# A two-layer decoder on one core: the fold of the second layer's experts moves into the end of the first layer's attention, and the gather of expert rows moves into the next stage's batch loop

## The chip, the cores and the metric

The kernel runs on one core of one Trainium2 chip. The core has TensorE (PE in the profile, with PEld for its weight loads), VectorE (DVE), ScalarE (ACT), GpSimd (POOL) and SyncE (SP, which here only issues DMAs). Each engine takes its instructions in the order of its own queue. The metric is the device time of one execution in microseconds (us).

## The reference, cut to what matters

Two decoder layers over x of 4 batches x 512 tokens x 256 channels, float32. Each layer is attention, cross attention, experts, each on a layer norm of x and added back to x:

```
x += L0_attn(LN(x))        # causal conv, 16 heads, cumulative memory
x += L0_xattn(LN(x), ctx)  # 16 heads, softmax over 512 keys
x += L0_ffn(LN(x))         # 12 experts, 2 per token: 8 with silu, 4 that pass x through
x += L1_attn(LN(x))        # gated scan over time: f = LN(x) @ W_f.T, scan, @ W_down.T
x += L1_xattn(LN(x), ctx)  # ternary weights, int8 activations
x += L1_ffn(LN(x))         # 8 linear experts, 2 per token: (x @ w_in[e].T) @ w_out[e].T
```

Two facts carry the change. The experts of the last line have nothing between their two matrices, so the product of w_in[e] (1024 x 256) and w_out[e] (256 x 1024) is a matrix of 256 x 256 that depends on weights alone; the kernel calls it the fold of expert e, and may compute it at any moment before the last stage. And the sum over a token's two experts in L0_ffn ends in a gather: each token fetches two rows out of a table in device memory and adds them, weighted by its shares, to its x.

## The kernel before, in words

Tokens lie on the 128 partitions, in 16 tiles (NT) of 128 tokens, 4 (QT) per batch. The stages run in the order of the list FAST: `l0_mixers` (both attentions of layer 0), `l0_gate`, `ahead`, `l0_experts`, `l1_attn`, `l1_xattn`, `l1_ffn`. A library orders the instructions of each engine when the kernel is built: it simulates the program, takes the first one in program order that is ready, and adds the waits. `keep_in_program_order` pins an instruction behind the one that was written before it for the same engine. Memory pools are handed out like a stack; what is put where another tile was waits until that tile's last use.

**l0_mixers.** After a prologue, a loop over 17 units u = 0..16 computes cross attention scores, four units to a batch. A unit has eight slots n = 0..7. In each slot `exponents` (from L912) does two score matmuls into one of two PSUM buffers, a DVE maximum (L917) and two ACT exponentials (L920), after which the buffer is free again. The dictionary `then` holds what is done behind each slot: for the unit before, `least` and `weigh` in slots 1 and 2 (small matmuls on PE, then DVE, ACT and a POOL product, L943), `gather_values` in slots 3 to 6 (eight `av` matmul instructions in each, which need that POOL product). SP fetches the next unit's keys and queries (`gather`, slot 0) and values (slot 4). The remaining slots of the first ten units do the first attention's work for later batches. In units 10 and 14 `project` puts one output projection (`xo`, eight matmul instructions of 128x256) in each of slots 4 to 7. Unit 16 has no scores; its tail is `collect` (the softmax sums go to device memory), `invert`, `give_back`, `spread` (eight DMAs and POOL products, L996) and `project` for batch 3, one behind the other. All matmuls here go through `pinned` and all SP DMAs through `move`, so PE and SP keep the written order. Single-bank PSUM tiles come from `ps_misc`, which has four banks.

**l0_gate.** Per batch: layer norm, turn, gate matmuls on PE, top two on DVE, and the row numbers; then POOL writes the normalized rows into the table by indirect DMAs (L1346), 32 in all.

**l0_experts.** `take(e)` loads an expert's weights and its 640 rows, `expert(e)` computes `ef` matmuls (shape 128x320, then 128x256) and writes the rows back (L1431). Beside it run `weights` (seven ternary weight matrices, DVE and SP), `images` (work for l1_xattn) and `fold` (L1710), a generator: for each of eight experts two 1 MB loads, 32 matmul instructions of 128x256, an ACT copy and a 256 KB write to `far_folded`. Its first steps are interleaved with `weights`, the rest are written last. Behind the experts stands the gather: for each of 16 tiles and two picks, an indirect DMA by POOL into `got` (six buffers, L1453) and one multiply-add into x on DVE (L1459).

**l1_attn.** For each batch: layer norm, eight PE transposes (`turn`), copies to `aht`; then for m = 0, 1, 2 four `f` matmuls (twice as many instructions, of 128x512), three ACT sigmoids, two DVE operations, a POOL product (L1531) and a DVE scan (L1532); then the `down` matmuls and the DVE addition to x (L1537).

**l1_ffn** reads `far_folded` near the end of the kernel.

Of the kernel before, what the change touches and what calls it, by code (L numbers as in the profile page):

```python
# [9 lines left out]
F32 = mybir.dt.float32  # L10
# [8 lines left out]
P = 128  # L19
# [521 lines left out]
def l0_mixers(k):  # L541
# [19 lines left out]
    k.close_psum()  # L561
    with ExitStack() as es:
        pool = lambda n, bufs, **kw: es.enter_context(tc.tile_pool(name=n, bufs=bufs, **kw))
        wp, wk, sp = pool("l0_w", 1), pool("l0", 2), pool("l0_s", 3)
        ps_misc, ps_s = pool("l0_misc", 4, space=PSUM), pool("l0_score", 2, space=PSUM)
# [26 lines left out]
        def load(name, src=None):  # L592
            src = a[name] if src is None else src
            t = wp.tile(list(src.shape), F32, name=f"{name}_sb")
            move(t, src)
            return t

        def load_rows(name):
            return load(name, a[name].rearrange("(c p) f -> p c f", p=P))

        def load_all(name):
            return load(name, a[name].to_broadcast([P, a[name].shape[1]]))
# [37 lines left out]
        gamma = wp.tile([16, 1], F32, name="gamma_sb")  # L640
# [10 lines left out]
        half_b = wp.tile([P, 4], F32, name="half_b")  # L651
# [12 lines left out]
        power = wp.tile([16, 10], F32, name="power")  # L664
        decay_of = []
        nought = wp.tile([1, P], BF16, name="nought")
        far_dec = dram.tile([2, 16, T], F32, name="far_dec", bufs=1)
        near_dec = wp.tile([P, 2, 64], F32, name="near_dec")
# [29 lines left out]
        cos = wp.tile([P, 4, T], F32, name="cos")  # L698
# [22 lines left out]
        def normalize(b):  # L721
            normal[b] = k.layer_norm(b)
            mixed[b] = wk.tile([P, DC, T], F32, tag="xc", name=f"xc_{b}", bufs=1)
# [24 lines left out]
        def measure(b, m):  # L748

            if m == 0:  # L750
                raw[b] = wk.tile([P, 4, T], F32, tag="qk", name=f"qk_{b}", bufs=1)
# [6 lines left out]
        heads = wp.tile([P, 4, 16], F32, name="heads")  # L758
# [16 lines left out]
        def scale_near(b):  # L775
            rn = near_of[b] = wk.tile([P, 3, 64], F32, tag="rn", name=f"rn_{b}", bufs=1)
# [13 lines left out]
        def factor(b, m):  # L790

            two = factor_of[b, m] = wk.tile([P, 2, T], F32, tag="factors", name=f"factors_{b}_{m}")
            by_channel(two, lambda r: factors[b][r, m])

        def gated_values(b, m):
# [6 lines left out]
            vg = gated[b, m] = wk.tile([P, T], F32, tag="vg", name=f"vg_{b}_{m}", bufs=4)  # L802
# [201 lines left out]

        def blank(n):
# [69 lines left out]
        w_o = load_rows("Wo")  # L1075
        b_o = load_all("bo")
# [49 lines left out]
        for u in range(units + 1):  # L1126
# [17 lines left out]
            near_b, next_b, last_b = b + 1, b + 2, b + 3  # L1144
            if m == 0:
# [59 lines left out]
        give_back(NB - 1)  # L1205
        for half in range(2):
            spread(NB - 1, half)
        for i in range(QT):
            project(NB - 1, i)
# [845 lines left out]
```

## Time and profile before

| what | us |
|---|---|
| median of 3 executions (lowest, highest) | 1324.41 (1321.67, 1333.49) |
| profiled execution, device time | 1339.99 |
| its span, first to last instruction | 1338.3 |
| l0_mixers, to the last `xo` matmul | 0 to 568 |
| gate and table writes, to the first expert matmul on rows | 569 to 646 |
| experts, to their last write of the table | 646 to 847 |
| gather of rows, to the first `f` matmul | 847 to 913 |
| rest of l1_attn | 913 to 1008 |
| l1_xattn and l1_ffn | 1008 to 1338 |

Of the span PE is busy 76%, DVE 61%, ACT 30%, POOL 16%; the mean granted PE clock is 0.847 of full speed. The 256 fold matmul instructions take 69.0 us of PE, the 32 gathers 31.1 us of POOL. A line of the profile names the source line, engine, operation, what is written and from what, and how many; in a timeline the first two numbers are the start and the duration in us, and the brackets hold the idle time before it and what ended that.

### The profile page before, as it was taken

How to read it: one execution, taken by the hardware profiler on the slowest of the kernel's cores; microseconds unless marked ns; L12 is line 12 of the kernel's file. 1: busy time of each engine (PE TensorE's matmuls, PEld its weight loads, DVE VectorE, ACT ScalarE, POOL GpSimd, SP SyncE). 2: the span in 40 equal slices, each digit the busy share in tenths (PEclk: the TensorE clock that was granted, in tenths of full speed). 3: DMA queues.
4: the chain of work that ended last, by engine and by line, in shares of the span. 5: the costliest groups of instructions: out<-in, count | busy, mean ns of one | idle time of the engine just before them, and what ended most of it. 6: DMA issues, size and time to landing. Idle time of an engine off the chain costs nothing. (4 is left out here: it accounts for less than half of the span.)

```text
span 1338.3 us, 11843 instructions
## 1 busy us (share of the span) xinstructions
PE 1015.5 (76%) x3742; PEld 559.0 (42%) x3742; DVE 812.9 (61%) x1969; ACT 405.0 (30%) x698; POOL 213.9 (16%) x245
## 2 busy tenths in 40 slices
PE   5859668789767667472689999849873788669996
PEld 2434323233323223262566677735441443255442
DVE  6646687787687666162356821254766555887564
ACT  4503246445434564010012321002311343730000
POOL 4421112112112010136000000451112110000000
PEclk9969778889887778665799999869986898979999
DMA  5382712524523230156565352651000011010000
GB/s 150 93 270 92 214 36 104 168 102 149 166 94 118 71 106 0 34 176 216 169 230 163 119 200 75 201 164 40 0 0 4 16 48 32 0 41 24 16 31 19
DMA packets 91885, 132.27 MB, mean 99 GB/s; under 512 B 20853, under 2 KB 62325, under 8 KB 91797
## 3 DMA queue, kind: packets, MB, share of 16 engines
q1 hardware_dynamic: 85648, 113.58, 27.2%
q0 software_dynamic: 6144, 17.83, 3.8%
q8 instruction: 32, 0.52, 0.2%
q14 instruction: 41, 0.33, 0.1%
q10 hardware_dynamic: 20, 0.00, 0.0%
HBM read 88.72 MB, written 42.66 MB: 98 GB/s over the span
## 5 line engine op out<-in xcount | busy, mean ns | idle before, releaser
L920 ACT ACTIVATE e<-score,tops 128x512 f32<-128x512 f32 x256 | 161.2, 685 | 152.0 <-DVE tops L917 103.2
L917 DVE TENSOR_REDUCE tops<-score 128x2 f32<-128x1024 f32 x128 | 155.6, 1220 | 50.5 <-PE score L581 49.8
L212 PE MATMUL y<-folded_sb,fht 128*128 128x512 f32 x256 | 113.0, 601 | 0.0
L581 PE MATMUL score<-query,key 64*128 64x512 f32 x256 | 73.2, 574 | 35.9 <-ACT e L920 34.1
L955 PE MATMUL av<-e,weighed 128*32 128x512 f32 x512 | 84.2, 700 | 19.7 <-POOL weighed L943 19.7
L1911 DVE SCALAR_TENSOR_TENSOR x_sb<-y,tt_w,x_sb 128x256 f32<-128x256 f32 x128 | 61.9, 483 | 38.5 <-PE y L212 34.9
L212 PE MATMUL ef<-sw,eact 128*128 128x256 f32 x320 | 79.9, 389 | 3.2 <-DVE ey L1429 3.2
L212 PE MATMUL fold<-w_out,w_in 128*128 128x256 f32 x256 | 69.0, 423 | 14.2 <-issue 14.2
L581 PEld LDWEIGHTS score<-query,key 64*128 64x128 f32 x256 | 27.2, 212 | 123.4 <-ACT e L920 71.8
L581 PE MATMUL o<-o_wT_sb,qk 128*128 128x256 f32 x128 | 51.0, 567 | 34.6 <-DVE qk L819 34.6
L212 PE MATMUL ef<-eht,sw 128*128 128x320 f32 x256 | 74.6, 435 | 0.6 <-ACT eact L1418 0.6
L212 PEld LDWEIGHTS y<-folded_sb,fht 128*128 128x128 f32 x256 | 48.9, 193 | 60.2 <-issue 60.2
L212 PEld LDWEIGHTS ef<-sw,eact 128*128 128x128 f32 x320 | 58.9, 194 | 13.9 <-DVE ey L1429 6.6
L212 PEld LDWEIGHTS fold<-w_out,w_in 128*128 128x128 f32 x256 | 53.8, 216 | 22.7 <-issue 15.0
L581 PEld LDWEIGHTS o<-o_wT_sb,qk 128*128 128x128 f32 x128 | 35.0, 287 | 49.7 <-DVE qk L819 40.0
L212 PEld LDWEIGHTS ef<-eht,sw 128*128 128x128 f32 x256 | 47.6, 190 | 18.4 <-ACT eact L1418 1.6
L1418 ACT ACTIVATE eact<-ef 128x640 f32<-128x640 f32 x32 | 22.4, 702 | 96.4 <-PE ef L212 96.3
L581 PE MATMUL xo<-Wo_sb,att 128*128 128x256 f32 x128 | 37.1, 439 | 16.8 <-POOL att L996 16.8
L212 PE MATMUL f<-aht,W_fT_sb 128*128 128x512 f32 x96 | 47.7, 645 | 1.4 <-DVE x_sb L1537 1.4
L1453 POOL DMA_INDIRECT got<-table,rows x32 | 31.1, 972 | 104.6 <-DMA table<-ey 94.2
L943 POOL TENSOR_TENSOR weighed<-v,weighed 128x256 f32<-128x256 f32 x16 | 10.5, 658 | 226.8 <-ACT weighed L942 226.8
L1398 PE MATMUL eturn<-ident,rows 128*128 128x128 f32 x80 | 16.9, 295 | 34.6 <-DMA rows<-table 30.8
(376 smaller groups left out, 1811.2 us busy)
## 6 DMA issues: line engine op xcount, KB each, us to landing
table<-zeros POOLq DMA_DIRECT2D x8, 1152.0 KB
factors<-far SPq DMA_DIRECT2D x64, 128.0 KB
key<-far_k SPq DMA_DIRECT2D x16, 512.0 KB
query<-far_q SPq DMA_DIRECT2D x16, 512.0 KB
w_in<-in_w_in SPq DMA_DIRECT2D x8, 1024.0 KB
w_out<-in_w_outT SPq DMA_DIRECT2D x8, 1024.0 KB
rows<-table SPq DMA_DIRECT2D x8, 640.0 KB
table<-ey SPq DMA_DIRECT2D x8, 640.0 KB
```

The source lines that it names most:

```text
L212: self.nc.tensor.matmul(out, lhs_t, rhs, start=(i == 0), stop=(i == len(pairs) - 1))
L581: nc.tensor.matmul(out, lhs_t, rhs, start=start and i == 0, stop=stop and i == len(pairs) - 1)
L917: nc.vector.tensor_reduce(top, ps, AX.X, ALU.max, negate=True)
L920: nc.scalar.activation(e[:, i, :], ps[:, i, :], AF.Exp, bias=top[:, i : i + 1])
L943: weighing[0] = nc.gpsimd.tensor_mul(wt[:, :, :, 0:16], vs[u], wt[:, :, :, 16:17].to_broadcast([P, QT, 4, 16]),)
L955: nc.tensor.matmul(avs[u][32 * h : 32 * h + 32, :], weighed[u % 2][:, j, h, :], es_of[u, h // 2, j][:, h % 2, :], start=(j == 0), stop=(j ...
L1398: nc.tensor.transpose(ps[:, c, :], rows[:, i, c * P : (c + 1) * P], k.ident)
L1418: nc.scalar.activation(act[:, f, :].rearrange("p (j t) -> p j t", j=2), ps[:, :, :half], AF.Silu)
L1453: nc.gpsimd.indirect_dma_start(out=got, out_offset=None, in_=k.table, in_offset=bass.IndirectOffsetOnAxis(ap=k.rows[:, which, t : t + 1], ...
L1911: nc.vector.scalar_tensor_tensor(xt, ps[:, e, :], w[:, i, e4 + e : e4 + e + 1], xt, ALU.mult, ALU.add)
```

## The change

Three things are done.

The fold leaves `l0_experts`. In `l0_mixers`, the tiles of the first attention now come from two pools of their own at the other end of the memory (`mw`, `mt`). At unit 10 (FOLDING) these pools are closed, and a pool `fold_w` for two experts' weights is opened in their place. A fold is cut into four pieces of eight matmul instructions; units 11 to 16 have one behind each of slots 0, 1, 2 and 7, which makes experts 0 to 5. Each fold's first piece also issues the next expert's loads, now four DMAs of 512 KB on SP; its last piece is followed by the ACT copy and the write to `far_folded`. Expert 6 comes behind `give_back` of the tail, expert 7 behind its last `project`. The pieces are pinned like the other matmuls and DMAs there.

The gather leaves `l0_experts`. In `l1_attn`, the 16 row fetches of the first two batches are issued at the start, and the four tiles of batch 0 are added to x before its layer norm. In batch b, behind m = 0 and m = 1, POOL issues the fetches for two tiles each of batch b + 2, and DVE adds two tiles each of batch b + 1. There are 16 `got` buffers instead of six. Fetches, additions and the POOL product are pinned.

`weights` in `l0_experts` is no longer interleaved with anything. The fold for the general path (not executed here) becomes a plain function.

```diff
 def l0_mixers(k):
+    far_folded(k)
+        mixers = ExitStack()
+        mw, mt = (
+            mixers.enter_context(tc.tile_pool(name=n, bufs=bufs, side="right"))
+            for n, bufs in (("l0_mix_w", 1), ("l0_mix", 2))
+        )
...
+        def fetch_fold(e):
+            folds[e] = []
+            for name in ("w_in", "w_outT"):
+                t = k.fold_w.tile([P, 8, D], F32, tag=name, name=f"{name}_{e}", bufs=2)
+                src = a[name][e].rearrange("(c p) d -> p c d", p=P)
+                for j in (0, 4):
+                    move(t[:, j : j + 4], src[:, j : j + 4])
+                folds[e].append(t)
+
+        def fold_piece(i):
+            e, c, j4 = i // 4, i // 2 % 2, i % 2 * 4
+            if i % 4 == 0:
+                folds[e].append(bank(f"fold_{e}").rearrange("p (c d) -> p c d", d=D))
+                if e + 1 < 7:
+                    fetch_fold(e + 1)
+            w_in, w_out, ps = folds[e]
+            pinned(
+                ps[:, c, :],
+                [(w_in[:, j, c * P : (c + 1) * P], w_out[:, j, :]) for j in range(j4, j4 + 4)],
+                j4 == 0,
+                j4 == 4,
+            )
+            if i % 4 == 3:
+                folded = k.fold_w.tile([P, DC * D], F32, tag="folded", name=f"folded_{e}", bufs=2)
+                nc.scalar.copy(folded.rearrange("p (c d) -> p c d", d=D), ps)
+                move(k.far_folded[e], folded)
...
             near_b, next_b, last_b = b + 1, b + 2, b + 3
+            if u == FOLDING:
+                mixers.close()
+                k.fold_pool = ExitStack()
+                k.fold_w = k.fold_pool.enter_context(tc.tile_pool(name="fold_w", bufs=2, side="right"))
+                after(7, fetch_fold, 0)
+            elif u > FOLDING:
+                for j, n in enumerate((0, 1, 2, 7)):
+                    after(n, fold_piece, 4 * (u - FOLDING - 1) + j)
...
         give_back(NB - 1)
+        for i in range(24, 28):
+            fold_piece(i)
         for half in range(2):
             spread(NB - 1, half)
+        fetch_fold(7)
         for i in range(QT):
             project(NB - 1, i)
+        for i in range(28, 32):
+            fold_piece(i)
+    k.fold_pool.close()
     k.open_psum()
...
 def l0_experts(k):
-        folding = fold(k, wf)
             ternary = weights(k, tw)
             take(0)
-            for _ in range(3):
-                for _ in range(2):
-                    next(folding)
-                    next(ternary)
...
-        for t in range(NT):
-            xt = k.x[:, t, :]
-            for which in range(2):
-                got = wk.tile([P, D], F32, tag="got", name=f"got_{t}_{which}", bufs=6)
-                nc.gpsimd.indirect_dma_start(out=got, ...)
-                nc.vector.scalar_tensor_tensor(
-                    xt, got, k.shares[:, which, t : t + 1], xt, ALU.mult, ALU.add
-                )
-        for _ in folding:
-            pass
...
 def l1_attn(k):
+        def fetch(t):
+            for which in range(2):
+                got[t, which] = wk.tile([P, D], F32, tag="got", name=f"got_{t}_{which}", bufs=16)
+                tc.keep_in_program_order(nc.gpsimd.indirect_dma_start(out=got[t, which], ...))
+        def add(t):
+            xt = k.x[:, t, :]
+            for which in range(2):
+                tc.keep_in_program_order(nc.vector.scalar_tensor_tensor(xt, got[t, which], ...))
+        for t in range(2 * QT):
+            fetch(t)
+        for t in range(QT):
+            add(t)
         for b in range(NB):
             h = k.layer_norm(b)
...
-                nc.gpsimd.tensor_mul(g, g, z)
+                tc.keep_in_program_order(nc.gpsimd.tensor_mul(g, g, z))
                 nc.vector.tensor_tensor_scan(state[:, m, :], fade, g, 0.5, ALU.mult, ALU.add)
+                for t in (2 * m, 2 * m + 1) if m < 2 else ():
+                    fetch((b + 2) * QT + t)
+                    add((b + 1) * QT + t)
```

## The prediction

> **What bounds the kernel now.** I read the granted clock first (0.847 on the one core), then busy time in stretches cut at the ends of units, stages and batches, then the timeline of each stretch that the diff touches, then its waits. The stretches, with the columns named in the first line:
>
> ```profile
> core 0: us, PE busy (x) PEld busy (x) DVE busy (x) ACT busy (x) POOL busy (x), PEclk, DMA share, GB/s
> ...
> 423.40:439.60 16.20, 16.20 (x81) 8.24 (x80) 10.77 (x17) 7.59 (x12) 0.23 (x1) 0.97 0.21 75
> ...
> 456.24:473.25 17.01, 11.44 (x53) 3.19 (x53) 10.47 (x13) 10.64 (x18) 0.64 (x1) 0.70 0.20 68
> ...
> 490.26:513.58 23.32, 19.13 (x84) 9.72 (x85) 13.84 (x23) 11.37 (x19) 3.10 (x3) 0.78 0.25 74
> ...
> 646.20:668.90 22.70, 20.57 (x86) 16.73 (x87) 8.78 (x28) 0.58 (x1) 0.00 (x0) 0.85 0.49 156
> ...
> 800.00:846.03 46.03, 46.03 (x205) 36.72 (x204) 8.53 (x17) 5.62 (x8) 0.00 (x0) 1.00 0.21 65
> 846.03:912.76 66.73, 43.54 (x175) 34.64 (x173) 32.66 (x128) 4.10 (x7) 31.10 (x32) 0.77 0.57 183
> ```
>
> The second row is a plain unit (12): 17.0 us, no engine full, PE at clock 0.70. The third is unit 14, with four projections. The experts (fifth) are all PE. The last row is the gather, where no engine is full: a chain. Its timeline:
>
> ```profile
> 846.49 0.36 SPq L1431 DMA_DIRECT2D table<-ey  x1
> 850.62 1.19 POOL L1453 DMA_INDIRECT got<-table,rows  x1 [94.22 <-DMA table<-ey]
> 856.14 0.48 DVE L1459 SCALAR_TENSOR_TENSOR x_sb<-got,shares,x_sb 128x256 f32<-128x256 f32 x1 [9.68 <-DMA got<-table,rows]
> ...
> 891.16 0.95 POOL L1453 DMA_INDIRECT got<-table,rows  x1 [0.30 <-issue]
> 897.48 0.48 DVE L1459 SCALAR_TENSOR_TENSOR x_sb<-got,shares,x_sb 128x256 f32<-128x256 f32 x1
> 904.23 7.81 PE L212 MATMUL fold<-w_out,w_in 128*128 128x256 f32 x32
> 912.76 7.13 PE L212 MATMUL f<-aht,W_fT_sb 128*128 128x512 f32 x16
> ```
>
> POOL issues 32 gathers from 850.62 to 892.1, one per 1.25 to 1.3 us; the first layer norm gets through DVE at 897, and a fold stands in front of the first `f`. So this stretch is paid for by the number of gathers, and the folds in it are only partly free.
>
> **Terms 1 and 2: gather and l1_attn.** The table's last write still lands at 850.6. Batch 0 now needs 8 gathers: the eighth is issued at 850.6 + 7 x 1.25 = 859.4. The first took 5.5 us to its use, beside 2 MB of fold loads which are gone; I take 4, bounds 3 and 5.5, so 863.4. Then addition 0.48, statistics 0.6, ten small operations of 0.2, four `h` of 0.34, turns 2.3, copy 0.7: `f` starts near 871 instead of 912.8. PE comes to it cold (it had been idle, not folding): I charge 2 us. **Term 1: -40.**
>
> From there l1_attn took 95.3 us (912.76 to 1008.03). The product of one m starts 4.03 us behind that of the m before (921.36, 925.40, 929.43). In batches 0 and 1 four gathers are pinned between two products on POOL: 1.27 + 4 x 1.25 = 6.27 us, 2.24 more, twice a batch, 9.0 in all. Behind the product wait the scan and, on DVE's queue, the next m. In batch 2 there are no gathers, but four additions of 0.48 behind the scan: 1.9, twice, 3.8. Layer norms 1 to 3 (about 5 us of DVE each, made beside the gathers before) also come in; DVE is busy about 15 of 22.6 us in a batch, mostly idle behind `down` (5.6 us), so I charge 1 us each. **Term 2: +16**, bounds +6 (only half of the gathers show) and +36 (all additions 11.5, three layer norms 16 and the gathers 9 in the chain).
>
> **Term 3: the experts start earlier.** Between 646.2 and 668.9 fold matmuls take 17.3 us of PE's 20.6. Expert 0's rows are turned by 654.7; its 32 `ef` matmuls were spread until 676.8. Without folds they take 9.2 us, some of them cold (+2): done at 666, 11 earlier. The ternary weights follow more slowly: a 1 MB fold load stood before W_f1's 2 MB load at 669, and the DVE passes over W_f1 (4.42, 2.35, 4.49) hold up the turns as now. I take **-9**. The gain lasts to the end because PE is then full (46.03 of 46.03 in the fifth row). Bounds 0 (weights hold everything) and -11.
>
> **Term 4: units 11 to 15.** Each gets 32 fold instructions, 128x256. The nearest row is the same shape, `xo`, first cold, then warm:
>
> ```profile
> 463.73 1.94 PE L955 MATMUL av<-e,weighed 128*32 128x512 f32 x8 [2.12 <-POOL weighed L943]
> ...
> 500.34 3.26 PE L581 MATMUL xo<-Wo_sb,att 128*128 128x256 f32 x8
> 503.53 1.07 PE L955 MATMUL av<-e,weighed 128*32 128x512 f32 x8
> 504.53 0.50 PE L581 MATMUL score<-query,key 64*128 64x512 f32 x2
> 504.96 1.99 PE L581 MATMUL xo<-Wo_sb,att 128*128 128x256 f32 x8
> ```
>
> A piece costs 2.0 us warm, 3.26 cold. In unit 12 PE idles 1.17, 0.96, 1.02 and 2.12 us behind slots 7, 0, 1 and 2: 5.3 us for 8. Slot by slot, at warm prices: behind 7, a score (0.43) and a piece make 2.45 where 1.67 was (+0.8); behind 0, 2.45 for 1.45 (+1.0); behind 1, with `low`, 2.72 for 1.72 (+1.0); behind 2 the piece hides in the wait for the weighed values (first line). A busier PE is also a faster one: in the stretch 423 to 440, PE full, the clock is 0.97, and `av` takes 1.07 instead of 1.94. The first two `av` groups and a score save 1.9. So +0.9 a unit for 11 to 13. Unit 14 has its projections behind slot 7 too: +3.1. Unit 15: +0.1. **Term 4: +6.** From below: all hidden, clock gain kept, -9. From above: unit 14's four projections lengthened it by 23.3 - 17.0 = 6.3 us; the same for each of five is +31. I stand nearer the lower end because the pieces sit in the idle slots, the projections in the full ones.
>
> [...]
>
> Loads: 2 MB per 17 us unit is 123 GB/s on top of at most 106 GB/s in these units; the stretch from 569 to 587 moved 244 GB/s, so 2 MB takes 8 to 9 us, and each expert is fetched a unit ahead. On SP the loads stand behind the next keys and queries (needed 17 us later) and before the values (needed later still). The first fetch has only its keep writes before it (427.8) and is not late at 440. Charged at nothing; if a load were late, every score behind the piece would wait.
>
> **Term 5: the tail.** Unit 16's gaps (1.63, 0.62, 1.37) take 3.6 of three pieces' 6: +2.2. Piece 23, its copy (0.6) and its 256 KB write are pinned before `collect`, whose DMA went out at 539.68: +2.6, and 1 for the queue. Expert 6's four pieces run while the sums travel (PE idles 12.7 us before 551.7), but its write is pinned before `spread`: +0.5. **+6.3**, bounds 0 and +13 (cold pieces).
>
> **Term 6: the gate.** Expert 7's 32 instructions stand before the gate's turns on PE if its loads are there: at that stretch's price (0.35 each, clock 0.56) 11.2 us, less what PE idles. Against that, fold 0 no longer delays batch 1's ranks, and POOL's gaps of 2.3 and 2.2 us between the table writes close: -4.5. The turns may also slip in between. **+3**, bounds -4.5 and +10.
>
> **Sum:** -40 + 16 - 9 + 6 + 6.3 + 3 = **-17.7 us** against the profiled execution's 1339.99 (span 1338.3). That execution was 15.6 us above the median shown; I carry the difference over: 1324.4 - 18 = **1306**.
>
> **Rivals.**
> *Everything goes well*: units hidden (0), gate -4, the experts -11, l1_attn +11: -40 + 11 - 11 + 0 + 6.3 - 4 = -38, 1286. The long idle of POOL and DVE in the gather speaks for it. Chance 0.15.
> *The experts do not move*: the weights' chain (loads, DVE) sets their pace, term 3 is 0: -9, 1315. For it: PE idled 4.7 us from 669 to 707 with W_f1 on DVE. Against it: from 800 on PE is full. 0.11.
> *The gather only moves*: layer norms and additions fall into the chain of l1_attn, term 2 is +31: -3, 1321. For it: additions are pinned behind the scan, and DVE is in order; against it: 5.6 us of DVE idleness behind `down` in each batch. 0.20.
> *Slower: pieces delay the scores.* PE's pinned queue makes each score wait for the piece before it. If each unit pays what unit 14 paid (6.3), term 4 is +31, and with cold pieces in tail and gate (+13, +10): -40 + 16 - 9 + 31 + 13 + 10 = +21, 1345. With tail and gate at those prices it decides from 4.6 us a unit (units of 21.6 us) that the kernel is slower by over 1%. Against it: unit 12's idle slots and the clock at 423 to 440. 0.14.
> *My sum*, 1296 to 1314: 0.40.
>
> **Numbers.** A measurement of this kernel tells about 1%, 13.2 us, from no change: borders 1311.2 and 1337.6. Faster: 0.15, 0.33 of my sum's 0.40, 0.04 of the third case: 0.52. Slower: 0.14. Within: 0.34. The range, 1284 to 1327, leaves out the slow case and the best end of the first, 0.18.
>
> **What would show it.** Units 11 to 13 near 18 us with a clock above 0.9; the collect DMA 10 to 12 us later in the span; POOL's table writes without gaps; PE's first long `ef` run over near 666 plus the delay so far; 16 gathers in a row, then `f` some 20 us behind the first; batches 0 and 1 of l1_attn at about 27 us. I am wrong if the units pass 21 us, if batches 1 and 2 pass 30 us, or if the table's last write does not come earlier relative to the gate.

## The result and the profile after

The changed kernel takes 1332.13 us (median of 20 runs, 1328.72 to 1341.11), the kernel before 1333.08 us (20 runs, 1321.67 to 1339.60); the ratio of the changed kernel to the one before is 1.0012, with a 95% interval of 0.9989 to 1.0035. **No difference can be measured**, where the forecast was 1306.

The two profiled executions are 1339.99 us (span 1338.3) and 1328.79 us (span 1327.1). Only a part of these 11.2 us belongs to the change: 3.7 us are there before the first changed unit starts and 4.0 us behind l1_attn, where nothing was edited. What lies between, cut at the same instructions in both traces:

| stretch | before | after | difference | forecast |
|---|---|---|---|---|
| units 11 to 13 | 50.7 | 50.3 | -0.4 | +2.7 |
| unit 14 | 23.3 | 33.2 | +9.9 | +3.1 |
| unit 15 (from one `low` turn to the next) | 16.3 | 15.5 | -0.8 | +0.1 |
| rest of the tail, to the last `xo` | | | +4.5 | +6.3 |
| last `xo` to the rows' DMA (gate) | 71.8 | 71.5 | -0.3 | +3 |
| rows' DMA to the last `ey` copy (experts) | 206.5 | 201.8 | -4.7 | -9 |
| last `ey` to the first gather | 4.6 | 4.8 | +0.2 | 0 |
| first gather to the first `f` | 62.1 | 18.1 | -44.1 | -42 |
| first `f` to the end of l1_attn | 95.3 | 127.4 | +32.1 | +18 |
| sum | | | -3.6 | -17.7 |

(The forecast charged 2 us of cold start to its first term; they are spent inside l1_attn, so they stand there. It rounded the three rows of units, 5.9, to 6. Small differences are not safe: over ten other kernels, below, that change nothing in the gate, it takes from 71.5 to 74.7 us, with one more at 76.5; l1_attn takes 127.0 to 129.7 in the seven kernels that have it as the changed kernel does.) The large gain is there, in its place and size. Two losses ate it: l1_attn and unit 14.

The busy time by stretches of the changed kernel, in the columns of its first line (length, busy time of each engine with its number of instructions, granted clock, DMA share, GB/s); the stretches are unit 11, unit 14, the gather, and the four batches of l1_attn:

```profile
core 0: us, PE busy (x) PEld busy (x) DVE busy (x) ACT busy (x) POOL busy (x), PEclk, DMA share, GB/s
435.92:452.86 16.94, 15.64 (x84) 8.16 (x83) 12.86 (x26) 10.66 (x19) 0.64 (x1) 1.00 0.58 185
486.24:519.44 33.20, 25.64 (x116) 14.20 (x115) 14.53 (x25) 12.51 (x22) 5.60 (x5) 0.90 0.50 144
851.02:873.46 22.44, 2.21 (x9) 1.48 (x9) 9.84 (x34) 0.06 (x1) 13.80 (x15) 0.55 0.35 106
873.46:908.65 35.19, 21.51 (x56) 11.61 (x56) 16.82 (x42) 7.68 (x12) 15.54 (x13) 0.75 0.14 42
908.65:942.33 33.68, 19.87 (x56) 11.27 (x56) 17.55 (x44) 6.12 (x11) 14.11 (x11) 0.80 0.11 31
942.33:971.90 29.57, 19.32 (x48) 10.74 (x48) 18.17 (x60) 5.78 (x10) 3.90 (x3) 0.83 0.00 1
971.90:1000.80 28.90, 22.33 (x77) 13.47 (x77) 21.17 (x65) 7.19 (x12) 3.83 (x3) 0.88 0.00 0
```

Unit 11 now carries 32 fold instructions and is as long as unit 12 was without them (17.01 us), with the clock at 1.00 instead of 0.70. Unit 14 is 10 us longer, although PE is busy only 6.5 us longer (19.13 before) at a higher clock (0.90, 0.78 before). In the last four rows no engine is full: the batches, 26.0, 22.5, 22.6 and 24.1 us before, are chains.

PE's timeline of the changed kernel in the gather and the first batch (start, duration, group, and in brackets the idle time before it and what ended it):

```profile
871.11 2.21 PE L203 MATMUL turn<-ident,h 128*128 128x128 f32 x8 [20.55 <-DVE h L190]
873.46 8.92 PE L212 MATMUL f<-aht,W_fT_sb 128*128 128x512 f32 x16
...
901.30 6.10 PE L212 MATMUL down<-W_downT_sb,state 128*128 128x256 f32 x20 [6.22 <-DVE state L1602]
...
909.40 10.54 PE L212 MATMUL f<-aht,W_fT_sb 128*128 128x512 f32 x24 [1.13 <-DVE aht L207]
```

The first `f` starts 39 us earlier in the span. But `down` waits 6.22 us for the last scan, and behind it all 24 `f` matmuls of batch 1 run in one go. In the kernel before, six of them had run ahead of `down`, and `down` had no such wait:

```profile
928.62 4.54 PE L212 MATMUL f<-aht,W_fT_sb 128*128 128x512 f32 x6
932.95 4.52 PE L212 MATMUL down<-W_downT_sb,state 128*128 128x256 f32 x20
```

POOL's timeline of the changed kernel shows what the scans wait for:

```profile
883.83 1.26 POOL L1601 TENSOR_TENSOR g<-g,z 128x512 f32<-128x512 f32 x1 [8.48 <-ACT fade L1595]
885.27 2.08 POOL L1559 DMA_INDIRECT got<-table,rows  x1 [0.18 <-issue]
887.65 0.95 POOL L1559 DMA_INDIRECT got<-table,rows  x1 [0.30 <-issue]
888.91 1.09 POOL L1559 DMA_INDIRECT got<-table,rows  x1 [0.30 <-DVE g L1600]
890.30 0.95 POOL L1559 DMA_INDIRECT got<-table,rows  x1 [0.30 <-issue]
891.27 1.27 POOL L1601 TENSOR_TENSOR g<-g,z 128x512 f32<-128x512 f32 x1
```

Two products stand 7.44 us apart. DVE's `g` was ready at 888.8; the four gathers in between held the second product until 891.27. In the kernel before they stand 4.03 us apart in batch 0, but 6.02 in batch 1:

```profile
921.36 1.27 POOL L1531 TENSOR_TENSOR g<-g,z 128x512 f32<-128x512 f32 x1 [29.26 <-DVE g L1530]
925.40 1.26 POOL L1531 TENSOR_TENSOR g<-g,z 128x512 f32<-128x512 f32 x1 [2.77 <-DVE g L1530]
...
941.93 1.27 POOL L1531 TENSOR_TENSOR g<-g,z 128x512 f32<-128x512 f32 x1 [11.23 <-DVE ln_half L169]
947.95 1.26 POOL L1531 TENSOR_TENSOR g<-g,z 128x512 f32<-128x512 f32 x1 [4.76 <-ACT g L1527]
```

### The profile page after: what moved, and what is told of

Same layout as the page of the kernel before. It is cut to its first block, busy times and chain, and to the rows that moved or that the text cites. A ratio compares the mean times of both kernels' runs of the same rounds, so it can differ in the third digit from the quotient of the medians.

```text
span 1327.1 us, 11827 instructions
## 1 busy us (share of the span) xinstructions
PE 988.3 (74%) x3735; PEld 547.3 (41%) x3742; DVE 811.8 (61%) x1969; ACT 405.7 (31%) x698; POOL 219.5 (17%) x245
## 5 line engine op out<-in xcount | busy, mean ns | idle before, releaser
L962 PE MATMUL av<-e,weighed 128*32 128x512 f32 x512 | 75.5, 629 | 12.4 <-POOL weighed L950 12.4
L588 PE MATMUL score<-query,key 64*128 64x512 f32 x256 | 66.2, 519 | 22.7 <-ACT e L927 20.9
L212 PE MATMUL ef<-eht,sw 128*128 128x320 f32 x256 | 77.4, 447 | 4.2 <-DVE eht L1457 3.8
L212 PE MATMUL down<-W_downT_sb,state 128*128 128x256 f32 x96 | 32.8, 499 | 38.3 <-DVE state L1602 34.7
L588 PE MATMUL fold<-w_outT,w_in 128*128 128x256 f32 x256 | 60.9, 386 | 0.0
L588 PEld LDWEIGHTS o<-o_wT_sb,qk 128*128 128x128 f32 x128 | 34.1, 280 | 50.0 <-DVE qk L826 40.7
L1559 POOL DMA_INDIRECT got<-table,rows x32 | 35.8, 1119 | 104.6 <-DVE neg_b L1551 95.8
L588 PEld LDWEIGHTS fold<-w_outT,w_in 128*128 128x128 f32 x256 | 46.8, 190 | 8.9 <-issue 3.3
L950 POOL TENSOR_TENSOR weighed<-v,weighed 128x256 f32<-128x256 f32 x16 | 10.5, 656 | 235.9 <-ACT weighed L949 215.0
L212 PE MATMUL f<-aht,W_fT_sb 128*128 128x512 f32 x96 | 44.2, 617 | 3.8 <-DVE aht L207 2.3
```

Source lines behind the costliest of these rows:

```text
L212: self.nc.tensor.matmul(out, lhs_t, rhs, start=(i == 0), stop=(i == len(pairs) - 1))
L588: nc.tensor.matmul(out, lhs_t, rhs, start=start and i == 0, stop=stop and i == len(pairs) - 1)
L950: weighing[0] = nc.gpsimd.tensor_mul(wt[:, :, :, 0:16], vs[u], wt[:, :, :, 16:17].to_broadcast([P, QT, 4, 16]),)
L962: nc.tensor.matmul(avs[u][32 * h : 32 * h + 32, :], weighed[u % 2][:, j, h, :], es_of[u, h // 2, j][:, h % 2, :], start=(j == 0), stop=(j ...
L1559: nc.gpsimd.indirect_dma_start(out=got[t, which], out_offset=None, in_=k.table, in_offset=bass.IndirectOffsetOnAxis(ap=k.rows[:, which, t ...
```

## The experiments

The theory after the traces, before the experiments: the change consists of a gather part that wins 44 us and gives 32 back inside l1_attn, and a fold part whose costs (a stall in unit 14, the tail) eat what it wins. The rivals were named run by run. Times are medians, ratios are to the kernel before on the same chip; the chips differ by some us (the kernel before took 1331.9, 1332.7, 1339.0 and 1332.4 us beside the four groups of runs).

### Each part alone

`fold_only` keeps the folds' new place and puts the gather back behind the experts:

```diff
 def l0_experts(k):
+        for t in range(NT):
+            for which in range(2):
+                got = wk.tile([P, D], F32, tag="got", ..., bufs=6)
+                nc.gpsimd.indirect_dma_start(out=got, ...)
+                nc.vector.scalar_tensor_tensor(xt, got, ...)
         psum.close()
 def l1_attn(k):
-        for t in range(2 * QT):
-            fetch(t)
-        for t in range(QT):
-            add(t)
...
-                    fetch((b + 2) * QT + t)
-                    add((b + 1) * QT + t)
```

> The fold part alone: folds in small steps in units 11 to 15, the tail and in front of the gate, while the 32 gathers stay in one block behind the experts with the last products in nobody's way. Theory (the parts cancel): against the kernel before, units and tail +13, gate 0, experts -5, and the block of gathers with the first `f` a few us shorter (no 2 MB of fold loads and no late fold in it, -2 to -8), so the kernel is within 1% of before, between -3 and +10 us; l1_attn's own 95 us does not change. Rival (the fold part is itself the gain and the gather part costs): 10 us or more faster than before.

Measured: 1331.51 us, ratio 1.0009 (0.9985 to 1.0032): as expected within 1%. Its PE timeline behind the experts:

```profile
899.56 0.69 PE L203 MATMUL turn<-ident,h 128*128 128x128 f32 x2 [46.18 <-DVE h L190]
...
903.03 8.52 PE L212 MATMUL f<-aht,W_fT_sb 128*128 128x512 f32 x16 [0.63 <-DVE aht L207]
```

PE idles 46 us there. From the first gather (858.16) to `f` it takes 44.9 us instead of 62.1, so 17 us of the 44 come from the folds having gone, more than the 2 to 8 us that I expected, and 27 from the gathers' new place. l1_attn takes 98.1 us, 2.9 more than before: the other 29 of the 32 us do not come from the folds. Unit 14 takes 33.0 us here too, and 23.2 in `gather_only`, next: its stall belongs to the fold part. Against `fold_only` the gather part brings -27 and +29: nothing.

`gather_only` is the kernel before with the changed l1_attn and without the gather in l0_experts; the five late folds stay behind the experts:

```diff
 def l0_experts(k):
-        for t in range(NT):
-            ...
         for _ in folding:
             pass
```

> The gather part alone: rows fetched a batch at a time in l1_attn, folds as in the kernel before (three beside the ternary weights, five behind the experts). Theory: the last five folds (160 instructions, some 38 us of PE beside 10 MB of loads) now stand in front of the first `f` with no gathers to lie beside, so `f` starts 30 to 40 us behind the experts instead of 18, and l1_attn pays its +32 as well: slower than before by 5 to 20 us. So neither part is worth anything without the other. Rival (the gather part is worth its 44 us by itself and l1_attn's loss comes from elsewhere): faster than before by 5 us or more.

Measured: 1359.96 us, ratio 1.0247 (1.0175 to 1.0318), 28 us slower in four executions, more than the 5 to 20 us that I expected. Its PE and POOL timelines behind the experts:

```profile
872.92 8.83 PE L212 MATMUL fold<-w_out,w_in 128*128 128x256 f32 x32 [2.55 <-DMA w_out<-in_w_outT]
```

```profile
885.53 1.19 POOL L1507 DMA_INDIRECT got<-table,rows  x1 [135.21 <-issue]
```

The last `ey` copy is at 839.92, but the first gather starts only at 885.53, 3.8 us behind the end of the last fold. So the folds now stand in a row in front of the gathers, and l1_attn takes 127.3 us, the same 32 us more. The loss in l1_attn belongs to the gather part, and the gather part needs the folds out of the way. (That the gathers waited for the memory of the fold weights is my reading of the gap; the trace only says "issue".)

### Unit 14: four kernels for two causes

In unit 14 `xo` waits for POOL's `att` products. PE's and SP's timelines of the changed kernel:

```profile
497.82 0.70 PE L588 MATMUL xo<-Wo_sb,att 128*128 128x256 f32 x2 [1.35 <-POOL att L1003]
...
504.59 2.44 PE L588 MATMUL xo<-Wo_sb,att 128*128 128x256 f32 x4 [4.85 <-POOL att L1003]
```

```profile
474.01 1.09 SPq L595 DMA_DIRECT2D w_in<-in_w_in  x2
475.15 1.69 SPq L595 DMA_DIRECT2D w_outT<-in_w_outT  x2
476.94 2.36 SPq L595 DMA_DIRECT2D sums<-far_sum  x1
489.09 0.34 SPq L595 DMA_DIRECT2D far_inverse<-sums  x1
```

The 2 MB of fold weights go out in front of the 32 KB read `sums`, and the write of its inverse follows at 489.09. Before, where no such load stood there, SP's line was

```profile
481.34 0.33 SPq L588 DMA_DIRECT2D far_inverse<-sums  x1
```

That is 8.9 us ahead of the start of unit 14 (490.26), against 2.9 us behind it (486.24) in the changed kernel. `sums_first` lets the read go first:

```diff
 def fold_piece(i):
-                if e + 1 < 7:
-                    fetch_fold(e + 1)
...
+            if u > FOLDING and u - FOLDING < 7:
+                after(0, fetch_fold, u - FOLDING)
```

> The changed kernel with one difference: in units 12 to 16 the 2 MB of fold weights are issued on SP behind the read of `sums` (slot 0's last step) instead of before it. Theory (the small read waits behind 2 MB in the queue): `fine` runs near 480 instead of 487.9 in the span, the attention products of the spread are ready before the projections, unit 14 goes from 33 back to 23 to 27 us and the kernel is 5 to 10 us faster than the changed one. Rival (PE's pieces, or the order in DVE's queue, hold up the spread): unit 14 stays at 31 us or more and the time does not change.

Measured: 1332.55 us, ratio 1.0016 (0.9982 to 1.0050), which is the rival's side of the expectation. The inverse went out at 484.08, 5 us earlier, and yet unit 14 took 32.3 us. POOL's timeline of this kernel shows why:

```profile
495.00 0.64 POOL L950 TENSOR_TENSOR weighed<-v,weighed 128x256 f32<-128x256 f32 x1 [16.05 <-ACT weighed L949]
495.59 2.50 POOL L1003 TENSOR_TENSOR att<-att,shares 128x512 f32<-128x512 f32 x2
502.42 2.48 POOL L1003 TENSOR_TENSOR att<-att,shares 128x512 f32<-128x512 f32 x2 [4.33 <-DMA shares<-far_inverse]
```

The first half of `att` follows `weighed` without a wait: it had been ready, but stood behind `weighed` in POOL's order, and the second half's `shares` use the same buffer. In the kernel before the first half stood in front of `weighed`:

```profile
487.06 2.51 POOL L996 TENSOR_TENSOR att<-att,shares 128x512 f32<-128x512 f32 x2 [6.39 <-DMA shares<-far_inverse]
497.06 0.64 POOL L943 TENSOR_TENSOR weighed<-v,weighed 128x256 f32<-128x256 f32 x1 [7.49 <-ACT weighed L942]
```

In the changed kernel and in `sums_first` the planner has swapped the two; that it did so because it counts on later `shares` is my reading. So two more kernels: `order_only` pins `att` in front of `weighed` in unit 13 and gives `shares` two buffers, `spread_free` does this and lets the read go first.

```diff
+            pool, bufs = (wk, 1) if b < 2 else (k.fold_w, 2)
-            shares = wk.tile([P, 2, T], F32, tag="shares", ..., bufs=1)
+            shares = pool.tile([P, 2, T], F32, tag="shares", ..., bufs=bufs)
...
-                nc.gpsimd.tensor_mul(att, att, shares[:, i, :])
+                tc.keep_in_program_order(nc.gpsimd.tensor_mul(att, att, shares[:, i, :]))
...
+            if u == 13:
+                tc.keep_in_program_order(weighing[0])
```

> The changed kernel with POOL's order and the two `shares` buffers of spread_free, but the fold loads in front of the read of `sums` as in the changed kernel. If POOL's order alone is the cause: unit 14 25 to 27 us as in spread_free. If the loads are a cause of their own: `fine` still runs near 488, `shares` go out at 490.6 and land 3 to 4 us later, both halves are multiplied by 497 to 500, and as `weighed` now stands behind them, unit 14 lies between: 27 to 31 us.

> The changed kernel with the read of `sums` in front of the fold loads (as in sums_first) and two more differences in the spread of units 13 and 14: on POOL the products `att` of the third frame's spread stand in front of the product `weighed` of unit 13 (in the changed kernel they stand behind it, in the kernel before the first half stood in front), and the third and fourth frames' `shares` have two buffers, so that the second half's read doesn't wait for the first half's product. Theory after sums_first (the planned order on POOL, not the loads by themselves, holds the second half until 503 us): both halves are multiplied by 497, the three waits of `xo` for `att` (1.35, 0.52, 4.85 us) go, unit 14 takes 25 to 27 us and the kernel is 5 to 8 us faster than the changed one. Rival (the reads of `shares` stand behind 2 MB of loads and land late whatever POOL does): `weighed` waits for them in its turn, unit 14 stays above 30 us.

Measured: `order_only` 1327.21 us, ratio 0.9988 (0.9958 to 1.0018), unit 14 34.1 us; `spread_free` 1320.20 us, ratio 0.9926 (0.9899 to 0.9953), unit 14 24.4 us. PE in `order_only`, then the stretch of unit 14 in `spread_free`:

```profile
502.86 1.94 PE L964 MATMUL av<-e,weighed 128*32 128x512 f32 x8 [8.29 <-POOL weighed L950]
...
505.45 3.68 PE L588 MATMUL xo<-Wo_sb,att 128*128 128x256 f32 x8
```

```profile
493.64:518.01 24.37, 23.01 (x116) 14.00 (x116) 13.91 (x21) 12.47 (x22) 5.55 (x5) 1.00 0.65 187
```

With the pinned order alone `weighed` waits for the late `shares`, and PE 8.29 us for `weighed`: the stall only moves, so my 27 to 31 us were too good. With the early read alone the order holds `att` back. Only both together make the stall go, to within 1.1 us of the 23.3 before. `spread_and_ln` and `all_four`, below, repeat this with 24.7 and 24.5 us. Each cause alone is enough to keep the stall, and both came with the fold part. What the pinned order does without the second `shares` buffer was not run; the kernel before had one buffer, the good order and no stall. `spread_free` gains another 5.4 us in the tail: the two `shares` buffers take away `xo`'s second wait there (4.29 us), which the kernel before had as well (4.13). `order_only` gains 4.0 us there in the same way, so this gain is not the cure of a loss that the change made.

### l1_attn: what the 32 us are made of

`gathers_behind` issues all eight gathers of batch b+2 behind the third product:

```diff
                 for t in (2 * m, 2 * m + 1) if m < 2 else ():
-                    fetch((b + 2) * QT + t)
                     add((b + 1) * QT + t)
+            for t in range(QT):
+                fetch((b + 2) * QT + t)
```

> The changed kernel with one difference: the 8 gathers of batch b+2 are issued in one go behind the third product of batch b, in the 17 us in which POOL has nothing to do, instead of four behind each of the first two products. Theory (POOL's gathers between products are half of l1_attn's loss): products of batches 0 and 1 stand 4.5 to 5.7 us apart instead of 7.45 (batch 2, without gathers, had 5.6 and 5.1), each of these two batches is 4 to 6 us shorter, the kernel 8 to 12 us faster than the changed one. Rival (DVE's additions and layer norms set the pace): the spacing stays above 6.5 us and the time gains under 4 us.

Measured: 1324.19 us, ratio 0.9967 (0.9934 to 0.9999); l1_attn 118.0 instead of 127.4 us. POOL's timeline:

```profile
882.92 1.27 POOL L1601 TENSOR_TENSOR g<-g,z 128x512 f32<-128x512 f32 x1 [7.28 <-ACT fade L1595]
888.02 1.37 POOL L1601 TENSOR_TENSOR g<-g,z 128x512 f32<-128x512 f32 x1 [3.83 <-DVE g L1600]
893.22 1.37 POOL L1601 TENSOR_TENSOR g<-g,z 128x512 f32<-128x512 f32 x1 [3.83 <-DVE g L1600]
```

Products 5.1 and 5.2 us apart, and now they wait for DVE's `g`. What the gathers between the products cost is 9.4 us. `ln_ahead` goes on from there: additions of b+1 in front of batch b's products, layer norm and turns of b+1 written behind its first scan.

```diff
+        prepare(0)
         for b in range(NB):
-            h = k.layer_norm(b)
-            ...
-            k.turned(h, lambda c: ht[:, c, :])
+            ht = hts[b]
+            if b + 1 < NB:
+                for t in range(QT):
+                    add((b + 1) * QT + t)
...
-                    add((b + 1) * QT + t)
+                if m == 0 and b + 1 < NB:
+                    prepare(b + 1)
```

> gathers_behind with a further difference: the eight additions of batch b+1 stand on DVE right behind the layer norm of batch b, in front of its first product, and the layer norm and turns of batch b+1 are written behind the first scan of batch b instead of behind its last step, so that `f` of b+1 can start before `down` of b is done. Theory (the other half of l1_attn's loss is that layer norm, turn and first `f` of each next batch no longer lie beside the batch before): batches of 24 to 27 us instead of 29 to 32, the kernel 8 to 15 us faster than gathers_behind. Rival (DVE is then the bound, with 3.8 us of additions and 5 us of layer norm more in each batch, and they delay the next `up`): gain under 4 us or a loss.

Measured: 1310.17 us, ratio 0.9853 (0.9811 to 0.9896); l1_attn 106.4 us, batches of 26 to 28 us. `adds_early` and `prepare_early` make the two halves of this edit alone.

> gathers_behind with the additions of batch b+1 in front of batch b's products instead of behind its first and second scan; the layer norm and turns of b+1 stay written behind the batch's last step. If the additions behind the scans are the dear part, the scans of one batch stand about 4 us apart instead of 5.2, and as the next batch's `x` is then ready early, the planner can also put the layer norm and turns beside the batch: a gain of 8 to 14 us on gathers_behind, as much as ln_ahead. If the written place of layer norm and turns is the dear part: under 4 us.

> gathers_behind with the layer norm and turns of batch b+1 written behind the second scan of batch b instead of behind its last step; the additions stay behind the first and second scan. If layer norm and turns behind `down` are the dear part: the 1.04 us turn and 1.13 us copy between `down` and the next `f` go, part of `f` runs before `down`, batches 3 to 4 us shorter, 8 to 12 us on gathers_behind. If the additions are the dear part: the layer norm only moves in front of the third `up`, and the gain is under 4 us.

Measured: `adds_early` 1319.01 us, ratio 0.9905 (0.9870 to 0.9940), l1_attn 110.8 us; `prepare_early` 1325.59 us, ratio 0.9955 (0.9929 to 0.9981), l1_attn 119.0 us. PE in `adds_early` at the end of batch 0:

```profile
896.55 2.84 PE L212 MATMUL f<-aht,W_fT_sb 128*128 128x512 f32 x6 [0.54 <-DVE up L1602]
899.95 4.58 PE L212 MATMUL down<-W_downT_sb,state 128*128 128x256 f32 x20 [0.55 <-DVE state L1605]
904.37 1.02 PE L212 MATMUL f<-aht,W_fT_sb 128*128 128x512 f32 x2
911.85 8.53 PE L212 MATMUL f<-aht,W_fT_sb 128*128 128x512 f32 x16 [6.46 <-DVE x_sb L1612]
```

With the rows added early the planner puts layer norm, turns and the first `f` of batch 1 beside batch 0 by itself; 7.2 us of the loss were the additions' place. The kernel gains 5 us on `gathers_behind`, less than the 8 to 14 expected. Layer norm and turns alone, written earlier, bring nothing, since they still need the late additions; on top of the early additions they bring the last 4.4 us (106.4 in `ln_ahead`, 104.0 and 106.5 in the two joined kernels below), by taking away waits like the 6.46 above.

`mul_on_dve` asks POOL's part in another way: the product on DVE, all 32 gathers in one go with a buffer each.

```diff
-                tc.keep_in_program_order(nc.gpsimd.tensor_mul(g, g, z))
+                nc.vector.tensor_mul(g, g, z)
...
-        for t in range(2 * QT):
+        for t in range(NT):
             fetch(t)
```

> The changed kernel with the product g*z on DVE instead of POOL, and all 32 gathers issued in one go on POOL, one buffer each; additions and layer norms stay as in the changed kernel. POOL is then out of l1_attn's chain altogether. Theory (POOL's queue is half of the loss): the scans of one batch stand 4 to 5.5 us apart, l1_attn takes 15 to 20 us less than the changed kernel's 127, the kernel is 13 to 20 us faster than the changed one. Rival (DVE is the pace): gain no more than gathers_behind's 8 us.

Measured: 1317.18 us, ratio 0.9891 (0.9857 to 0.9925), l1_attn 110.6 us, 17 us less than in the changed kernel: as expected, and 7 us more than the gathers' place alone. These 7 us need not be a part of the loss: in this kernel the product takes 0.69 us on DVE, against 1.27 on POOL, and there are 12 of them in the chain, about 7 us by estimate, which the kernel before paid as well.

### The experts and the last fold

`copies_on_act` moves the copies of the turned rows from DVE to ACT:

```diff
-                nc.vector.tensor_copy(ht[:, :, i * P : (i + 1) * P], ps)
+                nc.scalar.copy(ht[:, :, i * P : (i + 1) * P], ps)
```

> The changed kernel with one difference: in the experts' stage the copies of the turned rows from PSUM (`eht`, five an expert) run on ACT instead of DVE. In the changed kernel the experts' stage (first `eturn` to last `ey` copy) took 195.2 us against 199.8 before, although 17 us of fold matmuls had gone from PE: PE's idle time rose from 11.4 to 19.2 us, and its longest waits there are for `eht` on DVE (3.86, 3.23, 3.75). Theory (DVE, busy with the ternary weights, took over as the pace): these waits go, the stage takes 185 to 191 us and the kernel is 4 to 10 us faster than the changed one. Rival (the loads of the weights, or the chain of an expert itself, set the pace): the stage stays above 193 us and the kernel within 2 us of the changed one.

Measured: 1325.87 us, ratio 0.9896 (0.9861 to 0.9931). The experts' stage as a stretch in the kernel before, the changed one, and this one (columns as above):

```profile
646.23:846.03 199.80, 188.40 (x853) 142.28 (x854) 96.75 (x174) 42.00 (x59) 1.05 (x3) 0.97 0.46 150
```

```profile
655.40:850.60 195.20, 176.05 (x776) 129.75 (x780) 97.55 (x175) 41.29 (x57) 1.05 (x3) 0.95 0.40 129
```

```profile
663.45:844.40 180.95, 172.27 (x780) 127.67 (x780) 83.10 (x135) 54.99 (x97) 1.05 (x3) 0.97 0.44 139
```

The change took 12.3 us from PE here and got 4.6: PE's idle time rose from 11.4 to 19.2 us. With the copies off DVE it is 8.7 us, and the stage 14 us shorter, more than expected: 10.5 us of it are idle time of PE, the rest is PE itself, busy 3.8 us less with the same work. DVE is busy for only half of the stage (97.55 of 195.20); it was the place of the copies in its queue that PE waited for. Whether the same edit would help the kernel before, where PE idles 11.4 us, was not tried. (The gate took 5 us longer in this profile, from 71.5 to 76.5; in `all_four`, which has the same edit, it took 70.8. That is left open.)

`fold7_later` writes the last fold at the start of the experts' stage:

```diff
-        fetch_fold(7)
...
-        for i in range(28, 32):
-            fold_piece(i)
 def l0_experts(k):
+            fold(k, wf, (7,))
```

> The changed kernel with one difference: the last expert's fold, 32 instructions in front of the gate's first turn (7.07 us), is written at the start of the experts' stage instead, where PE waits 30 us for the first rows. Theory (those 32 instructions were the whole of the gate's delay): the first turn of the gate comes 6.5 to 7.5 us earlier behind the last `xo`, the rows are issued 5 to 7 us earlier, and the kernel is 4 to 7 us faster than the changed one. Rival (the fold then sits in front of the ranks or of expert 0's products, or its load of 1 MB in front of the rows): under 2 us faster.

Measured: 1334.09 us, ratio 0.9958 (0.9924 to 0.9991). In the changed kernel the fold stands in front of the gate's first turn:

```profile
577.14 7.07 PE L588 MATMUL fold<-w_outT,w_in 128*128 128x256 f32 x32
...
584.93 1.10 PE L203 MATMUL turn<-ident,gh 128*128 128x128 f32 x8 [0.60 <-ACT folded L1041]
```

Moved away, the first turn comes 1.5 us behind the last `xo` instead of 7.6, but from the last `xo` to the rows' DMA it takes 72.2 us instead of 71.5, so by the trace the rival is right: the planner put the fold between the gate's batches, and POOL's table writes have their gaps of 2.25 and 2.22 us again. The times do not settle it. The ratio, 0.9958 against the changed kernel's 1.0012, would be 7 us, but the two intervals just touch, and the stretch that was edited shows no gain.

### Together

`spread_and_ln` joins the edits of `spread_free` and `ln_ahead`; `all_four` adds those of `copies_on_act` and `fold7_later`.

> The changed kernel with the edits of spread_free and of ln_ahead (with the gathers of gathers_behind) together. They lie in different stages, so if both explanations hold their gains add up: 12 us and 22 us below the changed kernel's 1332, so 1295 to 1302. If part of either gain was the run-to-run difference of the first units, 1302 to 1310.

> spread_and_ln with copies_on_act and fold7_later on top. If each explanation holds by itself and no wait takes the place of the ones removed: a further 8 to 15 us, 1285 to 1294. If the last fold lands in front of expert 0 or ACT's copies hold up the experts' activations: no faster than spread_and_ln.

Measured: `spread_and_ln` 1298.87 us, ratio 0.9727 (0.9653 to 0.9801); `all_four` **1282.99 us, ratio 0.9599** (0.9529 to 0.9668). The explanations add up: `spread_and_ln` lies in the range of its expectation and `all_four` 2 us below its own. `all_four` beats both kernels by 4%, in four executions, with unit 14 at 24.5 us, the experts at 180.5 us and l1_attn at 106.5 us. Not all of this undoes losses of the change: the `shares` buffers cure a wait that the kernel before had too, and the copies' place may have cost it as well.

## Why the prediction was wrong, by its steps

**The base.** The forecast was 1324.4 - 17.7, from the median of three runs; over 20 runs the kernel before stands at 1333.1. The sum itself would have given 1315 from there; 8.7 us of the 26 us of error are the base. The stretches of the two traces make 14.1 (-3.6 against -17.7), which is as much as term 2 missed by. That the others cancel, the loss in unit 14 (+6.8) and in the experts (+4.3) against small gains in the rest, is luck. The last 3 us are the difference between the two traces and the medians, and rounding.

**Term 1 held**: -44.1 against -42, of which `fold_only` puts 17 down to the folds and 27 to the gathers, and the first `f` run, 8.92 us at a granted clock of 0.80 against 7.13 at 1.00, paid 1.8 of the 2 us charged for a cold start.

**Term 2 failed, +32 against +18** (its +16 and the 2 us of cold start). Its step of the gathers pinned between two products, 6.27 us apart and 9.0 in all, had the mechanism and two errors of size that cancel. The spacing was 7.44, since the first gather of each four took about 2 us, not 0.95; and without the gathers it is 5.1 to 5.2 (`gathers_behind`), not 4.03, which was read from batch 0 alone. That this part came out at 9.4 us, close to the 9.0, is luck. The failing step is the other one: "so I charge 1 us each" for the three layer norms, and 3.8 us for the additions of batch 2 alone, 6.8 us together. In batches 0 and 1 the additions stand behind the scans too; the next layer norm needs all of them, and so it, the turns and the next `f` came behind `down`. `adds_early` and `ln_ahead` give 7.2 and 4.4 us back, 11.6 together. Of the remaining 11 us, 2.9 are in `fold_only` too, 1.4 of them its first `f` run (8.52 us against 7.13). The cause of the other 8 stays open: DVE is busy 55.0 us in l1_attn before and 78.9 in `ln_ahead`, but also 73.7 in the changed kernel, which is 21 us slower there; and PE's clock is 0.83 in `ln_ahead` against 0.89 before, with PE busy 6 us longer. No run separates these. The case "the gather only moves" (term 2 at +31, forecast 1321) was the nearest by mechanism, and it stood at 0.20.

**Term 3 mis-sized, -4.7 against -9.** Its first step came out better than charged: the 32 `ef` matmuls of expert 0 end 16.3 us into the stage, and 30.6 before, 14 us earlier instead of 11. "The gain lasts to the end because PE is then full" is the step that failed. It looked at the last 46 us; in between PE waited for copies on DVE, as `copies_on_act` shows. The rival "the experts do not move" had named the weights' chain.

**Term 4: one part right, one step wrong.** Units 11 to 13 hid the pieces (-0.4 against +2.7), at 1.89 to 1.99 us each and with the clock at 1.00: the gain of a busier PE was larger than charged, as every `av` took 1.06 or 1.07 us and every pair of scores 0.49 to 0.51, while two `av` of unit 12 had taken 1.94 and 1.93 and four pairs of scores 0.77 to 0.80. The step on the loads, "Charged at nothing", failed in unit 14. It looked for late weights and late scores, and not for the small reads that stand behind the loads on SP: the 32 KB of `sums` and, after them, `shares`, on which POOL's products wait; and it did not ask whether the planned order on POOL would stay. Of the 9.9 us, `spread_free` gives back 8.8.

How long PE may wait before it comes back slower, no run shows; there are single cases. No piece of units 11 to 13 took the cold 3.26 us. In `order_only`, behind a wait of 8.29 us, `av` takes 1.94 and `xo` 3.68 us, while behind a wait of 0.85 us in the changed kernel's unit 14 `av` takes 1.06. In the prediction's row of unit 12 `av` takes 1.94 behind a wait of 2.12 us.

**Term 5 held**: +4.5 against +6.3. **Term 6** came out at -0.3 against +3, no more apart than profiles of the same gate: the fold's 7 us and the closed gaps between POOL's writes cancel, and `fold7_later` shows the two sides of it.

**The signs to look for** that the prediction named: clock above 0.9 in units 11 to 13, closed gaps in POOL's writes, expert 0's `ef` run over early, `f` about 20 us behind the first gather (18.1), all seen. The collect DMA came 12.6 us later relative to unit 11, near the 10 to 12 forecast, but by luck: 9.9 of it are unit 14. What was to be "batches 0 and 1 of l1_attn at about 27 us" was 35 and 34, past the 30 us at which I had called myself wrong for batch 1.

## What to carry to other kernels

When work leaves the critical path for the inside of a loop, price not only its own time there, but the prefetch that it destroys: what the next iteration had ready early now waits for the moved work (here six `f` matmuls of batch 1 that had run ahead of `down`). A load that is in time itself can still be dear to a small read behind it on the same queue (here 2 MB in front of 32 KB: the inverse went out 2.9 us behind the start of unit 14 instead of 8.9 ahead of it), and the planned order of another engine may change with it, so that curing one of the two brings nothing (unit 14 at 32.3 and 34.1 us, at 33.2 with neither cured and 24.4 with both); test both and their combination. And where work is taken from the busiest engine, look for what it will wait for next: here PE had 12.3 us less to do in the experts, and the stage became 4.6 us shorter.

## What the runs showed that was not expected

In most places of these traces a gather takes 0.94 or 0.95 us on POOL, but not everywhere. In `mul_on_dve` no POOL product is near the gathers, and yet those beside DVE's scans and products take longer, 1.09 to 2.16 us; POOL's and DVE's timelines of that kernel:

```profile
883.43 0.95 POOL L1559 DMA_INDIRECT got<-table,rows  x1 [0.30 <-issue]
884.68 1.22 POOL L1559 DMA_INDIRECT got<-table,rows  x1 [0.30 <-issue]
...
889.37 2.16 POOL L1559 DMA_INDIRECT got<-table,rows  x1 [0.30 <-issue]
```

```profile
889.57 1.21 DVE L1602 TENSOR_TENSOR_SCAN state<-fade,g 128x512 f32<-128x512 f32 x1
```

So the product on POOL is not needed for it. The 2.08 us of the first gather behind a product in the changed kernel lie beside a scan too (885.13 to 886.35), and the gather ends 1.0 us behind the scan, about a whole gather's 0.95. Not beside every DVE instruction are they longer: beside `up` and the first `g` (882.88 to 884.36) the gathers take 0.94 and 0.95 us, and beside the additions in the kernel before their median is 0.946. Nor is it the same beside every scan: in `mul_on_dve` a gather that starts at 886.21, in the middle of a scan (885.66, 1.21 us), takes 1.42 us, against the 2.16 above.

Some DVE operations are longer beside POOL as well. In the kernel before, three DVE operations on 128x4 values (`ln_u`, at 942.10, 964.64 and 987.26), 0.16 us long in the median, take 1.11 us each, and each ends within 0.03 us of the end of the POOL product that runs beside it. What decides which of the two takes longer, no run here tells.
